# One run of transposes between an expert's gate and up products

## The chip, the cores and the metric

The kernel runs on one core of a Trainium2 chip. The metric is the time of one execution on the device, in microseconds. The core has five engines that run side by side, each with a queue of its own that it works off in order: TensorE (PE; its weight loads have a row of their own, PEld), VectorE (DVE), ScalarE (ACT), GpSimd (POOL) and SyncE (SP). DMA engines move data between the memory of the chip and the core's own buffers. TensorE writes to PSUM, from where ACT and DVE read.

## The reference

The input has 8192 tokens of 512 numbers. It is normalised, and two things are added to it: a random-feature attention, which is two dense products with an exponential in between, and a mixture of experts with 64 experts, of which each token takes 8, and one shared expert.

```python
xn = layernorm(x)
# attention: random features of the tokens times those of the weights
feats = rfs(xn, xis, exp(xis), proj_matrix)
y = einsum('bsr,or->bso', feats, rfs(input_weights, xis, exp(xis), proj_matrix))
# experts: the first CAP = 256 tokens that chose expert e, in order
dispatch = zeros((E, CAP, h)).at[flat_e, pos_c].add(tokens[tidx] * valid[:, None])
g = einsum('ech,ehi->eci', dispatch, gate_w)
u = einsum('ech,ehi->eci', dispatch, up_w)
expert_out = einsum('eci,eih->ech', silu(g) * u, down_w)
output = zeros((t, h)).at[tidx].add(expert_out[flat_e, pos_c] * topk_w * SCALE * valid)
output += (silu(tokens @ shared_gate_w) * (tokens @ shared_up_w)) @ shared_down_w
return x + y + output
```

All of it is in float32. The gate and up weights of an expert are 512 x 256 each, the down weights 256 x 512.

## The kernel before

**Precision.** Each factor of a product is split in two: a high part that ACT makes as a rounded copy (`upper`, line 98), and a low part that DVE makes as the difference (`rest`, line 101). `products` (line 103) then issues three rounds of matmuls into the same PSUM tile: high by high, high weight by low value, low weight by high value. The low part of the weights is thus needed last, by the last third of the matmuls.

**Stages.** A first stage goes through the even blocks of 512 tokens: normalisation, transposes, routing, shared expert and attention. Then the loop over the experts begins (line 931). After it the last block and the shared expert of the odd blocks are computed (`ends`, line 892).

**The loop over the experts.** In step `i` the following is written down, in this order:

- the loads of the gate and up weights of expert `i+2` and of the down weights of `i+1` (SP);
- `hidden(i)` (line 792): the gate products, 48 matmuls of 256 columns, then the up products, 48 more, in PSUM tiles `ps_gu`; then `gated` (line 497), which is a tanh on ACT (499) and two multiplications on DVE (500, 501) into `sg`; then the split of `sg` into `ehT`;
- one step of `slots`, which finds the tokens of later experts; `gather(i+4)`, two indirect DMAs that POOL issues and that fetch the rows of that expert's 256 tokens into `xg`;
- `turn_slots(i+1)` (line 762): the 256 gathered tokens of the next expert are turned, in eight transposes of 128 x 128 on TensorE, in two halves with a PSUM tile `ps_t` each; ACT and DVE split each half into `gT`. Then DVE computes the tokens' shares `we` (781, 785);
- `split_gates(i+1)`: the gate and up weights of the next expert into `gu_h` and `gu_l`;
- some steps of `late_attention` (line 577), the attention of the odd blocks, which is put between the experts (tiles `ps_fu`, `ps_y`, `fU`, `yb`);
- `down(i-1)` (line 810): the down products of the expert before, in tiles `ps_e`, and the addition of its rows to the output by indirect DMA;
- `split_down(i)`.

**What sets the order.** The order in which the lines are written isn't the order in a queue. A scheduler puts the instructions of each engine in a fixed order when the program is built: earlier lines go first, but what it believes not to be ready is passed over for something later that is. The order can be bound by hand with `behind(a, b)` (line 117), which says that `a` comes after `b`, and adds no wait where both are on the same engine. The dictionary `last` keeps such instructions: `last["pe"]` is the newest matmul of `products`. In the kernel before, only the transposes of expert 0 are bound in this way.

**Buffers.** The tiles of 4 KiB per partition (weights, their parts, `gT`, `ehT`, `fU` and more) share a pool `four` of 40; `xg` has 4 buffers, `ps_t` 2, and `ps_gu` and `ps_e` share 4.

Of the kernel before, what the change touches and what calls it, by code (L numbers as in the profile page):

```python
# [22 lines left out]
E = 64  # L23
# [30 lines left out]
def rfs_attention_moe_kernel(  # L54
# [29 lines left out]
    def kib4(shape, name, dt=FPR):  # L84
        return four.tile(shape, dt, tag="four", name=name)
# [11 lines left out]
    def upper(dst, src):  # L97
        return nc.scalar.copy(dst, src)  # L98

    def rest(dst, src, hi, on=nc.vector):  # L100
        return on.tensor_tensor(dst, src, hi.bitcast(FP), ALU.subtract)  # L101

    def products(ps, w, v, start, stop):

        n = len(w)
        for part, (a, b) in enumerate(((0, 0), (0, 1), (1, 0))):
            for c in range(n):
                last["pe"] = nc.tensor.matmul(  # L108
                    ps,
                    w[c][a],  # L110
                    v[c][b],
                    start=(start and part == 0 and c == 0),
                    stop=(stop and part == 2 and c == n - 1),
                )
        return last["pe"]

    def behind(a, b):

        tc.add_manual_dep(a.ins, b.ins.name, ORDER, reason="what a needs comes late")
# [45 lines left out]
    last = {}  # L165
# [323 lines left out]
    def projected(v, rc, ps):  # L489
        products(ps, parts(pT, KC, ts(rc, P)), v, True, True)  # L490
# [6 lines left out]
    def gated(dst, g, u):  # L497

        nc.scalar.activation(dst, g, AF.Tanh, scale=0.5)
        nc.vector.scalar_tensor_tensor(dst, dst, 1.0, g, ALU.add, ALU.mult)  # L500
        nc.vector.scalar_tensor_tensor(dst, dst, 0.5, u, ALU.mult, ALU.mult)  # L501
# [9 lines left out]
    def attended(po, fT, s, start):  # L511

        return products(po, parts(fT, RC, ts(s, P)), parts(fW, RC), start, True)

    def dense(b, xT, whole, w, rows_of):
# [6 lines left out]
        for ic in range(IC):  # L522
            gu = []
            for n in range(2):
                ps = ps_mm.tile([P, TB], FP, tag="mm", name="ps_gu")
                wn = [(sgu_h[n][:, c, ts(ic, P)], sgu_l[n][:, c, ts(ic, P)]) for c in range(KC)]
                products(ps, wn, v, True, True)
                gu.append(ps)
            g, u = gu
            r = act.tile([P, TB], FP, tag="t", name="r")  # L530
            gated(r, g, u)
            upper(hT[0][:, ic, :], r)
            last["dve"] = rest(hT[1][:, ic, :], r, hT[0][:, ic, :])
            yield
# [111 lines left out]
    def split_gates(gu):  # L646
        return list(zip(*(split(t, "gu") for t in gu)))

    def split_down(d):
        return split(d, "d")  # L650
# [88 lines left out]
    def load_gates(e):  # L739
        gu = [kib4([P, KC, I], "gu", FP) for _ in range(2)]  # L740
        for t, w in zip(gu, (gw, uw)):
            nc.sync.dma_start(t, w[e].rearrange("(c p) i -> p c i", p=P))
        return gu

    def load_down(e):
        d = kib4([P, IC, H], "d", FP)
        nc.sync.dma_start(d, dw[e].rearrange("(c p) h -> p c h", p=P))
        return d

    def gather(e):  # L750
        xgs[e] = rows.tile([P, NH, XW], FP, tag="xw", name="xg")
        for h in range(NH):
            in_turn(
                nc.gpsimd.indirect_dma_start(  # L754
                    out=xgs[e][:, h, :],
                    out_offset=None,
                    in_=xnw,
                    in_offset=bass.IndirectOffsetOnAxis(ap=who[:, e, h : h + 1], axis=0),
                )
            )  # L760

    def turn_slots(e):
        xg = xgs.pop(e)
        xr = xg.bitcast(FPR)
        gp = [kib4([P, KC, CAP], "gT") for _ in range(2)]
        for c2 in range(KC // 2):
            pr = ps_tr.tile([P, 2, CAP], FPR, tag="tr", name="ps_t")
            ps = pr.bitcast(FP)
            for c in range(2):
                for h in range(NH):  # L770
                    turned_s = nc.tensor.transpose(  # L771
                        pr[:, c, ts(h, P)], xr[:, h, ts(c2 * 2 + c, P)], ident_r
                    )
                    if e == 0:
                        behind(turned_s, last["pe"])
            cs = slice(2 * c2, 2 * c2 + 2)
            upper(gp[0][:, cs, :], ps)
            turned_r = rest(gp[1][:, cs, :], ps, gp[0][:, cs, :])

        we = rt.tile([P, NH], FP, tag="we", name="we", bufs=4)  # L780
        shares = nc.vector.scalar_tensor_tensor(
            we, xg[:, :, H + e], 1.0, xg[:, :, H + E], ALU.add, ALU.mult
        )
        behind(shares, turned_r)
        nc.vector.reciprocal(we, we)
        wes[e] = we
        if e == 0:

            last["dve"] = shares
        return gp  # L790

    def hidden(e, gp, w):
        hi, lo = w
        v = [(gp[0][:, c, :], gp[1][:, c, :]) for c in range(KC)]
        gu = []
        for n in range(2):
            ps = ps_mm.tile([P, IC, CAP], FP, tag="mm", name="ps_gu")
            for ic in range(IC):
                wn = [(hi[n][:, c, ts(ic, P)], lo[n][:, c, ts(ic, P)]) for c in range(KC)]
                products(ps[:, ic, :], wn, v, True, True)  # L800
            gu.append(ps)
        g, u = gu
        sg = act.tile([P, IC, CAP], FP, tag="t", name="sg")
        gated(sg, g, u)
        hp = kib4([P, 2, IC, CAP], "ehT")
        upper(hp[:, 0], sg)
        last["dve"] = rest(hp[:, 1], sg, hp[:, 0])
        return hp

    def down(e, hp, w):  # L810
        dh, dl = w
        group = []
        ye = yes[e % len(yes)]
        for h in range(NH):
            po = ps_mm.tile([P, H], FP, tag="mm", name="ps_e")
            products(
                po,
                [(hp[:, 0, c, ts(h, P)], hp[:, 1, c, ts(h, P)]) for c in range(IC)],
                [(dh[:, c, :], dl[:, c, :]) for c in range(IC)],
                True,  # L820
                True,
            )
            nc.scalar.activation(ye[:, h, :], po, AF.Copy, scale=wes[e][:, h : h + 1])  # L823
            now = nc.gpsimd.indirect_dma_start(  # L824
                out=out,
                out_offset=bass.IndirectOffsetOnAxis(ap=who[:, e, h : h + 1], axis=0),
                in_=ye[:, h, :],
                in_offset=None,
                compute_op=ALU.add,
            )  # L830
            group.append(now)

        chain(group)
        in_turn(*group)

    xgs, wes, gps, gates, downs, gws, dws, hps = ({} for _ in range(8))
# [45 lines left out]
    for n in range(NS):  # L882
        next(rest_of)
        if n == 0:
            next(slots)
            gws[0] = split_gates(gates.pop(0))
    rest_steps -= RC + NS
    gps[0] = turn_slots(0)
    next(slots)
    yes = [kib4([P, NH, H], "ye", FP) for _ in range(3)]  # L890
# [40 lines left out]
    for i in range(E + 1):  # L931


        if i + 2 < E:
            gates[i + 2] = load_gates(i + 2)
        if i + 1 < E:
            downs[i + 1] = load_down(i + 1)
        if i < E:
            hps[i] = hidden(i, gps.pop(i), gws.pop(i))
        next(slots, None)  # L940
        if i + 4 < E:
            gather(i + 4)
        if i + 1 < E:
            gps[i + 1] = turn_slots(i + 1)
            gws[i + 1] = split_gates(gates.pop(i + 1))
        for _ in range(rest_steps * i // E, rest_steps * (i + 1) // E):
            next(rest_of, None)
        if i >= E - 2:
            next(last_of)
        if i == E:  # L950

            next(last_of)
        if i > 0:
            down(i - 1, hps.pop(i - 1), dws.pop(i - 1))
        if i < E:
            dws[i] = split_down(downs.pop(i))
            if i == E - 2:

                last["down"] = last["split"]
# [40 lines left out]
```

## Time and profile before

| what | value |
|---|---|
| time, median of 3 runs | 1310.99 us (1310.63 to 1311.27) |
| the profiled execution | 1310.94 us, of which 1309.2 are the span from the first to the last instruction |
| transposes `ps_t` (line 771) | 512, median 246 ns each, from 425.7 to 1130.7 us |
| copies `gT` on ACT (line 98) | 128, median 588 ns |
| subtractions `gT` on DVE (line 101) | 128, median 682 ns |
| gathers `xg` | 128, 3.5 to 10.1 us to landing, median 7.1 |
| data moved by DMA | 338.61 MB, mean 259 GB/s |

The profile is of one execution. A row of a timeline gives the start and the length in microseconds, the engine, the line of the code, the operation, the tile written and those read, the shapes and the count of instructions that follow each other. The matmuls overlap, so the lengths are longer than the pitch at which they start; where TensorE is the question, the starts are to be compared. A row for weight loads (PEld) belongs to the matmuls beside it. A line of waits names who waited, for whom, how long in total, how often and the longest. Line 108 is the matmul of `products` and lines 98 and 101 are `upper` and `rest`, for whatever tile they are called, so the tiles tell the rows apart.

### The profile page before, as it was taken

What the parts mean: (1) busy time and instruction counts of PE and PEld (TensorE: products, weight loads), DVE (VectorE), ACT (ScalarE), POOL (GpSimd) and SP (SyncE); (2) the same over time, 40 slices, a digit from 0 to 9 for tenths busy, and PEclk for the clock granted to TensorE, in tenths of its full rate; (3) what the DMA queues carried; (4) which work ended last, traced back from release to release, by engine and by line L of the source; (5) the groups of instructions that cost most, each with busy time, mean ns of one, the idle gap of its engine ahead of it and who ended that gap; (6) DMA issues with size and microseconds to landing.
All of it is one profiled execution on the core that took longest, in us unless ns stands there. A gap on an engine that the chain in (4) does not pass through costs nothing.

```text
span 1309.2 us, 21368 instructions
## 1 busy us (share of the span) xinstructions
PE 1296.7 (99%) x7648; PEld 1138.6 (87%) x7648; DVE 925.0 (71%) x1922; ACT 645.2 (49%) x1017; POOL 581.7 (44%) x692
## 2 busy tenths in 40 slices
PE   8999999999999999999999999999999999999998
PEld 6888888888888999999999999999999999988886
DVE  7978768867865776777767677776776676643555
ACT  5643544354432555656566556555665566540111
POOL 3122022123106767877666667767676654210000
PEclk9999999999999999999999999999999999999999
DMA  7665675675586989999999999999999999784995
GB/s 255 242 213 205 244 279 199 238 286 212 201 307 193 317 226 330 259 290 272 304 282 266 292 272 274 246 321 262 282 256 303 280 261 233 206 239 168 318 319 193
DMA packets 189498, 338.61 MB, mean 259 GB/s; under 512 B 15952, under 2 KB 87632, under 8 KB 189392
## 3 DMA queue, kind: packets, MB, share of 16 engines
q1 hardware_dynamic: 153456, 245.93, 54.6%
q0 software_dynamic: 35936, 91.32, 29.7%
q8 instruction: 60, 0.98, 0.3%
q14 instruction: 46, 0.38, 0.1%
HBM read 220.66 MB, written 104.99 MB: 249 GB/s over the span
## 4 chain that ended last, share of the span: by engine, by line
PE 91%; DVE 4%; DMA 2%; SPq 1%; ACT 1%; issue 1%; POOL 0%; DVEq 0%; ACTq 0%
PE ps_gu L108 41%; PE ps_e L108 13%; PE ps_o L108 13%; PE ps_y L108 6%; PE ps_fu L108 6%; PE ps_f L108 4%; PE ps_t L771 3%; PE ps_x L331 2%; PE ps_l L364 2%; DMA xb<-in_L_attn_x_dram 1%; DVE st L275 1%; DMA xT_l<-turned 1%; SPq L262 1%; DVE xT_l L101 1%; DMA gu<-in_L_ffn_up_w_dram 0%
## 5 line engine op out<-in xcount | busy, mean ns | idle before, releaser
L824 POOL DMA_INDIRECT out_dram<-ye,who x128 | 225.3, 1760 | 189.3 <-ACT ye L823 140.9
L108 PE MATMUL ps_gu<-gT,gu_h 128*128 128x256 f32 x2048 | 290.0, 283 | 0.0
L108 PEld LDWEIGHTS ps_gu<-gT,gu_h 128*128 128x128 f32 x2048 | 267.2, 191 | 5.6 <-ACT gu_h L98 1.0
L701 POOL DMA_INDIRECT at<-upto,line x128 | 138.0, 1078 | 76.0 <-DVE first_of L695 37.3
L108 PE MATMUL ps_gu<-gT,gu_l 128*128 128x256 f32 x1024 | 167.0, 285 | 0.0
L101 DVE TENSOR_TENSOR gu_l<-gu,gu_h 128x1024 fp32r<-128x1024 f32 x128 | 155.7, 1218 | 6.9 <-ACT gu_h L98 6.9
L754 POOL DMA_INDIRECT xg<-xnw,who x128 | 137.3, 1073 | 39.0 <-issue 32.0
L108 PE MATMUL ps_e<-d_h,ehT 128*128 128x512 f32 x512 | 148.5, 391 | 0.0
L108 PEld LDWEIGHTS ps_gu<-gT,gu_l 128*128 128x128 f32 x1024 | 140.7, 191 | 0.3
L98 ACT CAST gu_h<-gu 128x1024 fp32r<-128x1024 f32 x128 | 132.4, 1058 | 0.0
L98 ACT CAST ehT<-sg 128x512 fp32r<-128x512 f32 x64 | 39.7, 621 | 156.3 <-DVE sg L501 156.3
L823 ACT ACTIVATE ye<-ps_e,we 128x512 f32<-128x512 f32 x128 | 88.6, 694 | 57.0 <-PE ps_e L108 56.1
L108 PEld LDWEIGHTS ps_e<-d_h,ehT 128*128 128x128 f32 x512 | 94.7, 188 | 18.8
L246 POOL TENSOR_TENSOR a<-rstd,ve 128x4 f32<-128x4 f32 x45 | 10.5, 233 | 200.1 <-DVE rstd L242 197.6
L501 DVE SCALAR_TENSOR_TENSOR sg<-sg,ps_gu 128x512 f32<-128x512 f32 x64 | 43.9, 686 | 68.4 <-PE ps_gu L108 68.0
L507 ACT ACTIVATE f<-f,ab 128x512 f32<-128x512 f32 x64 | 46.3, 723 | 82.0 <-DVE f L493 81.3
L101 DVE TENSOR_TENSOR d_l<-d,d_h 128x1024 fp32r<-128x1024 f32 x64 | 78.2, 1222 | 7.8 <-ACT d_h L98 7.4
L101 DVE TENSOR_TENSOR gT<-ps_t,gT 128x512 fp32r<-128x512 f32 x128 | 83.2, 682 | 0.2 <-ACT gT L98 0.2
L101 DVE TENSOR_TENSOR ehT<-sg,ehT 128x512 fp32r<-128x512 f32 x64 | 44.3, 692 | 51.5 <-ACT ehT L98 51.5
L108 PE MATMUL ps_o<-fW_h,fT 128*128 128x512 f32 x288 | 80.0, 392 | 0.2 <-ACT fT L98 0.2
L108 PE MATMUL ps_e<-d_l,ehT 128*128 128x512 f32 x256 | 79.3, 391 | 0.0
L108 PE MATMUL ps_o<-d_h,hT 128*128 128x512 f32 x256 | 79.1, 396 | 0.0
(181 smaller groups left out, 2526.8 us busy)
## 6 DMA issues: line engine op xcount, KB each, us to landing
gu<-in_L_ffn_gate_w_dram SPq DMA_DIRECT2D x64, 512.0 KB
gu<-in_L_ffn_up_w_dram SPq DMA_DIRECT2D x64, 512.0 KB
d<-in_L_ffn_down_w_dram SPq DMA_DIRECT2D x64, 512.0 KB
xnw<-xw SPq DMA_DIRECT2D x32, 577.0 KB
xb<-in_L_attn_x_dram SPq DMA_DIRECT2D x32, 512.0 KB
out_dram<-xb SPq DMA_DIRECT2D x32, 512.0 KB
xT_h<-turned SPq DMA_DIRECT2D x30, 512.0 KB
xT_l<-turned SPq DMA_DIRECT2D x30, 512.0 KB
```

The lines of the kernel that those rows point to most:

```text
L98: return nc.scalar.copy(dst, src)
L101: return on.tensor_tensor(dst, src, hi.bitcast(FP), ALU.subtract)
L108: last["pe"] = nc.tensor.matmul(ps, w[c][a], v[c][b], start=(start and part == 0 and c == 0), stop=(stop and part == 2 and c == n - 1),)
L331: last["turn"] = nc.tensor.transpose(pr[:, ts(s, P)], src(s)[:, ts(kc, P)], ident if dt is FP else ident_r)
L364: logits = nc.tensor.matmul(pl, rwp[:, kc].rearrange("p t e -> p (t e)"), v[kc], start=(n == 0 and kc == 0), stop=(n == 1 and kc == KC - 1),)
L501: nc.vector.scalar_tensor_tensor(dst, dst, 0.5, u, ALU.mult, ALU.mult)
L507: nc.scalar.activation(f, f, AF.Exp, scale=ab[:, rc : rc + 1])
L701: nc.gpsimd.indirect_dma_start(out=at[:, e % TE, h, :], out_offset=None, in_=upto, in_offset=bass.IndirectOffsetOnAxis(ap=line[:, e, h : h ...
L754: nc.gpsimd.indirect_dma_start(out=xgs[e][:, h, :], out_offset=None, in_=xnw, in_offset=bass.IndirectOffsetOnAxis(ap=who[:, e, h : h + 1], ...
L771: turned_s = nc.tensor.transpose(pr[:, c, ts(h, P)], xr[:, h, ts(c2 * 2 + c, P)], ident_r)
L823: nc.scalar.activation(ye[:, h, :], po, AF.Copy, scale=wes[e][:, h : h + 1])
L824: now = nc.gpsimd.indirect_dma_start(out=out, out_offset=bass.IndirectOffsetOnAxis(ap=who[:, e, h : h + 1], axis=0), in_=ye[:, h, :], in_o ...
```

## The change

`turn_slots(e + 1)` is called from within `hidden(e)`, between the gate and the up products, and no longer from the loop. The first of its eight transposes is bound behind the last gate product; its last one is kept in `last["run"]`, and the next matmul that `products` issues, which is the first up product, is bound behind it. With the transposes the copies and subtractions of `gT` and the shares `we` are written down at the earlier place, ahead of `gated`. For expert 0, only the first transpose is now bound behind the product before it, and not all eight.

```diff
@@ products
                     stop=(stop and part == 2 and c == n - 1),
                 )
+                if "run" in last:
+                    behind(last["pe"], last.pop("run"))
         return last["pe"]
@@ turn_slots
                     turned_s = nc.tensor.transpose(
                         pr[:, c, ts(h, P)], xr[:, h, ts(c2 * 2 + c, P)], ident_r
                     )
-                    if e == 0:
+                    if c2 == c == h == 0:
+
                         behind(turned_s, last["pe"])
             cs = slice(2 * c2, 2 * c2 + 2)
             upper(gp[0][:, cs, :], ps)
             turned_r = rest(gp[1][:, cs, :], ps, gp[0][:, cs, :])
+        last["run"] = turned_s
@@ hidden
             gu.append(ps)
+            if n == 0 and e + 1 < E:
+                gps[e + 1] = turn_slots(e + 1)
@@ the loop over the experts
         if i + 1 < E:
-            gps[i + 1] = turn_slots(i + 1)
             gws[i + 1] = split_gates(gates.pop(i + 1))
```

## The prediction

> **What bounds the kernel.** First the page: the busy shares, the clock row and the chain of waits.
>
> ```profile
> span 1309.2 us, 21368 instructions
> PE 1296.7 (99%) x7648; PEld 1138.6 (87%) x7648; DVE 925.0 (71%) x1922; ACT 645.2 (49%) x1017; POOL 581.7 (44%) x692
> ...
> PEclk9999999999999999999999999999999999999999
> ...
> PE 91%; DVE 4%; DMA 2%; SPq 1%; ACT 1%; issue 1%; POOL 0%; DVEq 0%; ACTq 0%
> ```
>
> TensorE sets the end, at its full clock, so a microsecond counts only if it leaves TensorE's queue. Next the windows, cut where the experts begin and end (columns: length, busy time and count of each engine, granted clock, DMA share, GB/s):
>
> ```profile
> 0.00:427.00 427.00, 419.94 (x2058) 348.22 (x2058) 322.70 (x1018) 189.34 (x354) 104.69 (x331) 1.00 0.67 237
> 427.00:1142.00 715.00, 715.00 (x4883) 658.05 (x4883) 517.18 (x780) 424.05 (x615) 470.81 (x358) 1.00 0.98 275
> 1142.00:1309.20 167.20, 161.73 (x710) 132.29 (x708) 85.14 (x124) 31.77 (x49) 6.20 (x4) 0.99 0.74 243
> ```
>
> The change acts in the middle stretch alone (64 experts, about 11.9 us each), where TensorE shows no idle time at all. The time left to gain hides in the pitch of its instructions, from start to start. From the timeline I take the usual pitch: 227 ns for a matmul of 512 columns, 120 ns for one of 256. At these prices, and 84 ns per transpose (below), everything TensorE starts in this stretch comes to 707.3 us of its 714.9: only about 7.6 us are lost, and the change can't win more.
>
> **The price of a run.** TensorE's timeline around experts 18 and 19 (start, length, what, count):
>
> ```profile
> 631.62 0.64 PE L108 MATMUL ps_gu<-gT,gu_l 128*128 128x256 f32 x4
> 632.10 0.80 PE L771 MATMUL ps_t<-ident_r,xg 128*128 128x128 f32 x8
> 632.74 1.16 PE L108 MATMUL ps_y<-fW_h,fU 128*128 128x512 f32 x4
> 633.74 1.08 PE L108 MATMUL ps_y<-fW_l,fU 128*128 128x512 f32 x4
> ...
> 638.28 1.12 PE L108 MATMUL ps_gu<-gT,gu_h 128*128 128x256 f32 x8
> 639.24 0.46 PE L771 MATMUL ps_t<-ident_r,xg 128*128 128x128 f32 x4
> 639.53 0.72 PE L108 MATMUL ps_gu<-gT,gu_l 128*128 128x256 f32 x4
> ```
>
> Eight transposes start at 632.10 and the next row at 632.74: 80 ns each. But the four matmuls behind them take 1.00 us to the next row, where four at 227 ns take 0.91. Leaving a run costs something: the first matmul behind it holds the queue for about 300 ns instead of 227 (or 190 instead of 120), while the first two transposes of a run are cheap (60 ns each).
>
> I counted the rows of ps_t from 425.9 to 1131 us: 111 for 64 experts (32 of eight, 41 of four, 16 of two, 10 of one, 8 of three, 2 of six, 2 of seven). For each I took the time from its first transpose to the fifth matmul after its end, less 120 or 227 ns per matmul. A straight line through these gives 84 ns per transpose plus 51 ns per run. Over 84 ns each, the 111 runs lose 5.84 us in all: an eight followed by 512 columns 56 ns (32 of them, 1.80 us), a four followed by 256 columns 22 ns in the median (358 ns in all), the rest being waits that fall into the same places. What is lost away from the runs is 1.75 us.
>
> **The change, part by part.** Nothing is computed that wasn't before: 512 transposes, 128 copies and 128 subtractions stay. No DMA is moved and nothing passes SP's or POOL's queue.
>
> *The runs.* With the transposes of expert e+1 fixed behind the gate products of e and ahead of its up products, 111 runs become 64. An eight followed by 256 columns isn't in the trace. By the four that is followed by 256 columns it is 358 + 4 x 84 = 694 ns, 22 over; by the eight followed by 512 columns it is 56 over. So the 64 lose 1.4 to 3.6 us, and the gain is 5.84 - 1.4 = 4.4 to 5.84 - 3.6 = 2.2 us. I take 22 ns, as what follows a run sets the price of leaving it and in the new place 256 columns follow; rounded, **4.3 us**.
>
> *The cover that goes.* In 23 experts a run of one half stands just ahead of the gate's first use of gu_l (639.24 above), and that is no accident. VectorE's timeline there:
>
> ```profile
> 636.97 1.28 DVE L101 TENSOR_TENSOR gT<-ps_t,gT 128x512 fp32r<-128x512 f32 x2
> 638.17 0.15 DVE L781 SCALAR_TENSOR_TENSOR we<-xg 128x2 f32<-128x2 f32 x1
> 638.24 1.22 DVE L101 TENSOR_TENSOR gu_l<-gu,gu_h 128x1024 fp32r<-128x1024 f32 x1
> ```
>
> The weights' low half is ready at 639.46, after the run began at 639.24: the transposes fill a wait of 0.22 us. Over the 23 these waits sum to 2.6 us, and some 0.06 us of hand-over each makes 4.0. The new order bars transposes there. Two ends: it costs 4.0 us if the split stays as late, and it wins up to 0.9 us, the uncovered waits that nine other experts show at this place (six of 41 to 82 ns) or at the gate's first products (three of about 180 ns), if the splits come earlier. I take 0: the three VectorE rows ahead of the split (1.28 + 0.15, all of the transposed tokens) move some 3 us forward with the transposes (the second half of a run starts 3.0 us or more behind the gate's last product in most experts), far more than the longest wait.
>
> *The moved copies.* Two ACT copies (588 ns each) and on VectorE two subtractions (682), the shares (152) and the reciprocal (157) come before the gate and up results are used: 1.67 us of VectorE per expert. The view of waits says what room there is:
>
> ```profile
> ACT ehT L98 <- DVE sg L501: 151.2, 57, 3.1
> ...
> DVE sg L501 <- PE ps_gu L108: 64.9, 51, 1.6
> ACT sg L499 <- PE ps_gu L108: 62.9, 49, 3.5
> ...
> DVE ehT L101 <- ACT ehT L98: 50.7, 58, 3.7
> ...
> DVE sg L500 <- ACT sg L499: 32.8, 25, 2.7
> ```
>
> VectorE idles 64.9 + 32.8 + 50.7 = 148 us here, 2.3 per expert, most of it while up is computed, which is when the moved work now comes. Where it doesn't fit, L500 and L501 are late by up to 0.7 us, and after them ehT; the down products that read it stand an iteration (11.9 us) later, so nothing on TensorE waits. Cost 0; without that cover it would be 0.7 us an expert.
>
> *The new waits.* Up products now stand behind the transposes in TensorE's queue, and behind up the late attention and the down products. The transposes wait for the gather of e+1, whose second half is issued at least 14.6 us (mostly 21 to 31) before the gate ends, against 3.5 to 10.1 us to landing. Expert 1 alone has 8.3 us: 0 by the median landing of 7.1, 1.8 us once by the longest. I take 0. The two gT buffers are held up to 3 us longer, out of 40 that the weight loads draw on as well; those loads are issued 17.6 us or more, mostly 20 to 30, ahead of their first use, so a delay of 3 us leaves 14: 0.
>
> [...] The trace holds 32 runs of eight already, and the clock in three of them, looked at alone, is 1.00, their pitch 80 to 88 ns. [...]
>
> The sum: the span goes from 1309.2 to 1304.9; the profiled execution took 1310.94 with what lies around the span, the median is 1310.99, so 1310.99 - 4.3 = **1306.7 us**.
>
> **Rivals.** *The split comes early and its waits go too:* 4.3 + 0.9 = 5.2, so 1305.8; for it, VectorE's new slack; against it, that the fixed order of its queue may use the slack otherwise. *A wait takes the gain's place:* the 23 covered waits come into the open for 4.0 us, or other work still falls between the transposes (only the first of them and the first up product are tied), so that there are as many runs as before: 1310.7 to 1311. For it, half of the splits end within 0.2 us of their use. *Slower:* VectorE executes in order; the subtractions of gT now wait for transposes, and what is queued behind them (yb, d_l, gu_l) waits as well. If the gate's low half then waits in every expert as long as in the 22 where it was late (2.6/22 + 0.06 = 0.18 us), that is 11.5 us against 4.3: 1318.2. It decides from (4.3 + 2.6)/64 = 0.11 us per expert on. Against it: 72% load on VectorE in this stretch, and work that moves forward rather than back.
>
> **How the numbers follow.** Forecast 0.40 (its own range 1306.0 to 1308.8), early split 0.17, gain eaten 0.25, slower 0.18. A measurement of this kernel can tell 0.2%, 2.6 us. The first two are faster but for a corner of the forecast's range: 0.55; the third is no change, with that corner 0.27; slower 0.18. The range takes in the first three: from 1304.5 (the 7.6 us of all losses, less the 1.4 that 64 runs keep, is 1304.8) to 1313.0 (the third with expert 1's wait of 1.8).
>
> **What would show it.** Right: about 64 rows of ps_t with eight each, each after a gate's last row; TensorE still without idle time; gu_l ending well ahead of its use; the stretch of the experts about 4 us shorter. Wrong: rows of ps_t in pieces; matmul pitches over 200 ns where gu_l begins; waits of TensorE for VectorE or for gathers, in the waits or the chain.

## The result and the profile after

The changed kernel takes 1309.28 us (median of 22 runs, 1307.85 to 1310.75) where the kernel before took 1311.12 in runs beside it: the ratio is 0.9985 (0.9979 to 0.9992), a gain of some 2 us. A second comparison gave 0.9989 (0.9982 to 0.9995). The gain is smaller than the 0.2% that the prediction called the least a measurement can tell, but both intervals exclude no gain at all. The forecast was 4.3 us, 1306.7. So the sign was right, and more than half of the expected gain is missing. The time lies outside the forecast's own range (1306.0 to 1308.8) and inside the whole range (1304.5 to 1313.0) only because that one also took in a gain that is eaten up.

One number of the kernel's description has to be corrected first: the gate products of an expert are 24 matmuls and the up products 24, not 48 each. From here on the line numbers are those of the kernel that is shown; they shift by a few lines from one to the next.

The page of the changed kernel:

```profile
span 1308.0 us, 21401 instructions
PE 1295.1 (99%) x7648; PEld 1136.1 (87%) x7648; DVE 925.9 (71%) x1922; ACT 644.1 (49%) x1017; POOL 587.0 (45%) x692
```

The profiled execution took 1309.75 us, 1.2 less than the one of before; the pair of profiles thus shows less than the medians do. The experts' stretch, cut at its own ends (window, length, busy and count of each engine, clock, DMA), before and then changed:

```profile
427.10:1141.90 714.80, 714.80 (x4882) 657.88 (x4882) 517.09 (x780) 423.95 (x615) 470.77 (x357) 1.00 0.98 275
427.50:1140.80 713.30, 713.24 (x4883) 655.49 (x4883) 518.00 (x780) 422.88 (x615) 475.94 (x358) 1.00 0.98 276
```

The kernel before took 714.8 us for one instruction of TensorE less. The order that the change asked for is there. TensorE's timeline around one turn of the changed kernel:

```profile
541.84 0.64 PE L108 MATMUL ps_gu<-gT,gu_l 128*128 128x256 f32 x4
542.32 0.80 PE L773 MATMUL ps_t<-ident_r,xg 128*128 128x128 f32 x8
```

There are 64 rows of ps_t, each of eight, and each but expert 0's stands right behind a gate's last product. By the measure of the prediction (84 ns a transpose, 120 or 227 a matmul; what the stretch takes beyond that is lost) the losses divide so:

| lost in the experts' stretch, us | before | changed |
|---|---|---|
| at the runs of transposes | 5.84 (111 runs) | 2.09 (64 runs) |
| away from them | 1.75 | 4.25 |
| sum | 7.59 | 6.34 |

The places of the runs gave 3.75 us. Not all of that is the price of a run: before, the medians (50 ns where 512 columns follow, 75 runs; 25 ns where 256 do, 36 runs) come to 4.65 us, and the other 1.2 us were waits that fell into the same places. And 2.5 us came back somewhere else. The timeline of TensorE shows where, at the start of expert 10's gate in the changed kernel:

```profile
538.54 0.39 PE L108 MATMUL ps_y<-fW_h,fU 128*128 128x512 f32 x1
538.89 1.22 PE L108 MATMUL ps_gu<-gT,gu_h 128*128 128x256 f32 x8
539.95 0.63 PE L108 MATMUL ps_y<-fW_h,fU 128*128 128x512 f32 x2
```

A matmul of 512 columns holds the queue for 0.227 us, but the gate starts 0.35 us after it, and its eight products take 1.06 us to the next row, not 0.96. That is 0.23 us lost, though no row of TensorE is marked as idle: the wait sits in the weight loads. What they wait for is on ACT:

```profile
532.23 1.07 ACT L98 CAST gT<-ps_t 128x512 fp32r<-128x512 f32 x2
536.70 0.69 ACT L830 ACTIVATE ye<-ps_e,we 128x512 f32<-128x512 f32 x1 [3.40 <-PE ps_e L108]
537.28 0.61 ACT L98 CAST ehT<-sg 128x512 fp32r<-128x512 f32 x1
537.79 1.05 ACT L98 CAST gu_h<-gu 128x1024 fp32r<-128x1024 f32 x1
```

The high half gu_h of the gate's weights is done at 538.84, and the gate starts 0.05 us later. ACT could have made it long before: it stood idle for 3.40 us at ye, the scaled copy of the down products, waiting for ps_e, with ehT and gu_h queued behind. The loads aren't what it waits for; they are issued 18 us or more ahead of their use, as before. Counted at every gate's first products, such waits come to 2.3 us in 13 experts; before they were 0.65 us in four, and some more inside the places of the runs. In nine experts of the changed kernel a ye stands between the copies gT and the gate's gu_h, as here; seven of them have a wait of 0.23 us.

The view of waits says the same in sums (who, for whom, total, times, longest). Before:

```profile
ACT ye L823 <- PE ps_e L108: 53.2, 41, 4.8
...
DVE gu_l L101 <- ACT gu_h L98: 6.9, 25, 0.9
...
PEld ps_gu L108 <- ACT gu_h L98: 1.0, 3, 0.3
```

Changed:

```profile
ACT ye L830 <- PE ps_e L108: 81.3, 54, 5.9
...
DVE gu_l L101 <- ACT gu_h L98: 13.4, 44, 0.9
...
PEld ps_gu L108 <- ACT gu_h L98: 4.7, 15, 0.4
```

ACT waits half as long again for ps_e, and what needs gu_h waits more for it. Of the waits that the prediction wanted to use as room, the two around ehT are smaller, while VectorE waits no less for ps_gu; so a part of the room was used, but in an order that puts ye ahead. In the changed kernel:

```profile
ACT ehT L98 <- DVE sg L503: 112.0, 44, 2.8
...
DVE sg L503 <- PE ps_gu L108: 72.0, 59, 2.3
...
DVE ehT L101 <- ACT ehT L98: 26.1, 27, 1.9
```

### The profile page after: what moved, and what is told of

Its sections match the earlier page's. It is cut to its first block, busy times and chain, and to the rows that moved or that the text cites. A ratio compares the mean times of both kernels' runs of the same rounds, so it can differ in the third digit from the quotient of the medians.

```text
span 1308.0 us, 21401 instructions
## 1 busy us (share of the span) xinstructions
PE 1295.1 (99%) x7648; PEld 1136.1 (87%) x7648; DVE 925.9 (71%) x1922; ACT 644.1 (49%) x1017; POOL 587.0 (45%) x692
## 4 chain that ended last, share of the span: by engine, by line
PE 87%; DVE 7%; DMA 3%; SPq 1%; issue 1%; ACT 1%; POOL 0%; ACTq 0%; DVEq 0%
PE ps_gu L108 41%; PE ps_e L108 13%; PE ps_o L108 12%; PE ps_fu L108 6%; PE ps_y L108 5%; PE ps_t L773 3%; PE ps_f L108 3%; PE ps_x L333 2%; PE ps_l L366 1%; DMA xb<-in_L_attn_x_dram 1%; DVE st L277 1%; DVE f L495 1%; SPq L264 1%; DVE xT_l L101 1%; DVE fT L101 1%
## 5 line engine op out<-in xcount | busy, mean ns | idle before, releaser
L831 POOL DMA_INDIRECT out_dram<-ye,who x128 | 232.7, 1818 | 181.5 <-ACT ye L830 120.8
L703 POOL DMA_INDIRECT at<-upto,line x128 | 131.9, 1030 | 76.0 <-DVE first_of L697 37.3
L756 POOL DMA_INDIRECT xg<-xnw,who x128 | 141.7, 1107 | 40.0 <-issue 30.0
L501 ACT ACTIVATE sg<-ps_gu 128x512 f32<-128x512 f32 x64 | 38.2, 597 | 77.7 <-PE ps_gu L108 77.7
```

The source lines that it names most:

```text
L703: nc.gpsimd.indirect_dma_start(out=at[:, e % TE, h, :], out_offset=None, in_=upto, in_offset=bass.IndirectOffsetOnAxis(ap=line[:, e, h : h ...
L756: nc.gpsimd.indirect_dma_start(out=xgs[e][:, h, :], out_offset=None, in_=xnw, in_offset=bass.IndirectOffsetOnAxis(ap=who[:, e, h : h + 1], ...
L831: now = nc.gpsimd.indirect_dma_start(out=out, out_offset=bass.IndirectOffsetOnAxis(ap=who[:, e, h : h + 1], axis=0), in_=ye[:, h, :], in_o ...
```

## The experiments

The theories, by the letters used below. A: each run of transposes has a price, which depends on what follows it. C (against it): the gain comes from the copies and subtractions that moved forward. D: what is missing is the gate's wait for gu_h behind ye on ACT. B and I: what is laid in front of gu_l, transposes (B) or late attention (I), covers a wait. E, F, G, H and J are the rivals that the expectations name. Each comparison is with the kernel before, run beside it on the same chip.

### The weights' wait

**e4_gate_before_ye**: the changed kernel, ye bound behind the high half of the next gate's weights, on ACT.

```diff
+        last["high"] = both[0]
...
-        return list(zip(*(split(t, "gu") for t in gu)))
+        gate = split(gu[0], "gu")
+        last["gate_high"] = last["high"]
+        return list(zip(gate, split(gu[1], "gu")))
...
-            nc.scalar.activation(ye[:, h, :], po, AF.Copy, scale=wes[e][:, h : h + 1])
+            behind(
+                nc.scalar.activation(ye[:, h, :], po, AF.Copy, scale=wes[e][:, h : h + 1]),
+                last["gate_high"],
+            )
```

> The changed kernel with one tie more on ACT: the copies ye of the down products come behind the high half of the next gate's weights. Theory D: ACT no longer stands idle for ps_e with gu_h queued behind; the waits of the gate's first products go, 2.3 us less than the changed kernel, about 1307. Rival E: the wait is only moved, since ye comes later and with it the PSUM of the down products: 1309 or more.

Measured: 1306.04 us, ratio 0.9965 (0.9952 to 0.9979). ACT at the same expert:

```profile
534.30 0.62 ACT L98 CAST ehT<-sg 128x512 fp32r<-128x512 f32 x1 [2.78 <-DVE we L792]
534.83 1.04 ACT L98 CAST gu_h<-gu 128x1024 fp32r<-128x1024 f32 x1
535.77 0.69 ACT L834 ACTIVATE ye<-ps_e,we 128x512 f32<-128x512 f32 x1
```

gu_h is now done at 535.87, 0.9 us ahead of the gate (536.75). ye starts 1.0 us ahead of the gate and no longer 2.2, and no new loss shows that would come from it. The sums of the waits follow:

```profile
ACT ye L834 <- PE ps_e L108: 40.2, 42, 2.3
...
PEld ps_gu L108 <- ACT gu_h L98: 0.3, 1, 0.3
```

The losses away from the runs fall from 4.25 to 1.33 us, those at the runs stay (1.81), and the stretch loses 3.1 us in all. Theory D holds for the changed kernel.

**e11_tie_again** and **e12_change_again**: the same kernel and the changed kernel side by side on one chip.

> The changed kernel with the ACT tie once more, beside the changed kernel on the same chip: by theory D 2.5 to 3.5 us below it.

> The changed kernel once more, as the base of the other three: 1.5 to 2.3 us below the kernel before, as it was measured.

Measured: 1306.11 us, 0.9968 (0.9956 to 0.9979), and 1308.87, 0.9989 (0.9982 to 0.9995). The intervals don't meet: the tie is worth 2.8 us, as expected.

**e5_before_tie**: the tie on the kernel before.

> The kernel before with the ACT tie alone (ye behind the next gate's high half), the transposes left where they were. Theory D (the tie mends a wait that the change brought in): before has only some 0.6 us of waits at the gate's first products, and its 111 runs stay, so 0 to 1 us less, 1310 to 1311. Rival F (the tie is worth as much without the change): 3.5 us less, as it was on the changed kernel, about 1307.

Measured: 1310.68 us, 0.9999 (0.9991 to 1.0007), with 113 runs of transposes and 7.7 us lost in the stretch. The tie alone is worth nothing there, and rival F falls. The order on ACT says why: before, a ye stands between gT and gu_h in two experts alone, so there was next to nothing for this tie to move. (In eight experts of that kernel gu_h is ready less than 0.1 us ahead of the gate as well, always with gT, not ye, straight ahead of it; against 13 in the changed kernel.)

**e3_weights_too**: the split of the next gate and up weights at the new place as well.

```diff
                 gps[e + 1] = turn_slots(e + 1)
+                gws[e + 1] = split_gates(gates.pop(e + 1))
...
-        if i + 1 < E:
-            gws[i + 1] = split_gates(gates.pop(i + 1))
```

> The changed kernel with the split of the next expert's gate and up weights moved to the same place, behind the transposes. Theory D (what was not gained is the gate waiting for its weights' high half, which ACT makes late because it stands idle in order): the waits at the gate's first products, 10 experts with 0.23 us each, and at its first use of gu_l, go: 2 to 3 us less than the changed kernel, about 1307. Rival E (the waits only move: ACT and VectorE come late with sg and the shared buffers are held longer): no gain or some loss, 1309 to 1312.

Measured: 1306.91 us, 0.9975 (0.9967 to 0.9983). It mends the wait in another way: the losses away from the runs are 1.74 us, and in 63 of 64 experts nothing stands in front of the gate's first gu_l any more, since the split is early. **e8_weights_and_tie**, both together:

> The changed kernel with both repairs, the weights' split at the earlier place and the ACT tie. Theory D: both mend the same wait, so the two together give little more than the tie alone: 1305.5 to 1306.5. Rival: they mend different waits and add up, 1303.5 to 1304.5.

Measured: 1307.08 us, 0.9974 (0.9963 to 0.9985); losses of 1.73 us away from the runs, as in e3. They don't add up, as they would if they mended different waits. The time is slightly above the expected range. The tie alone has the lowest median, but the intervals of e3, e4, e8 and e11 overlap.

### The price of a run

**e10_eight_runs**: on e4, the transposes one by one, each behind three gate products. The last has the place that it has in one run and the others are earlier, so nothing can come late for it.

```diff
...
+                if turning is not None and (part * n + c) % 3 == 2:
+                    next(turning, None)
...
```

> The changed kernel with the ACT tie, and the eight transposes one by one, each behind three gate products, the last behind the gate's last: every transpose is earlier than in one run, so none of the work behind them can be late for it. Theory A (leaving a run has a price of about 20 ns over, by the medians of the twos, fours and eights followed by 256 columns): 512 x 20 ns = 10.2 us instead of 1.6, so 8 to 9 us over the kernel with the tie (1306.0), 1314 to 1315. Rival H (runs have no price, the gain was waits): 1306 to 1307.

Measured: 1316.48 us, 1.0049 (1.0036 to 1.0063), 10.4 above e11. TensorE's timeline:

```profile
605.62 0.52 PE L108 MATMUL ps_gu<-gT,gu_h 128*128 128x256 f32 x3
605.98 0.22 PE L778 MATMUL ps_t<-ident_r,xg 128*128 128x128 f32 x1
606.04 0.57 PE L108 MATMUL ps_gu<-gT,gu_h 128*128 128x256 f32 x3
606.45 0.22 PE L778 MATMUL ps_t<-ident_r,xg 128*128 128x128 f32 x1
```

From 605.98 to 606.45 there are 0.47 us for one transpose and three matmuls, which alone take 0.36: 0.11 us for a transpose, where 84 ns is the price within a run. The 504 runs of one lose 12.4 us, 24.6 ns each; a run of eight followed by 256 columns loses 25.6 in the changed kernel. So leaving a run has the same price for one as for eight. Away from the runs only 1.25 us are lost. Theory A holds, rival H falls; so does C as the only cause, since here the copies come no later and the time rises with the number of runs. The expected 8 to 9 us were a little low, as I had taken 20 ns.

**e7_four_runs**: on e4, four runs of two, behind each quarter of the gate and up products.

> The changed kernel with the ACT tie, and the eight transposes in four runs of two, one behind each quarter of the gate and up products. Theory A (each run has a price): 256 runs instead of 64; by the twos of before 21 to 27 ns over for those followed by 256 columns, 30 to 50 for those followed by 512, so about 3 x 24 + 40 = 112 ns per expert instead of 26: 5.5 us more than the kernel with the tie (1306.0), 1311.5. Rival H (a run has no price of its own, the gain was waits): no more than 1 us over 1306.

Measured: 1318.41 us, 1.0055 (1.0041 to 1.0068), some 12 above e4 and 7 above theory A's number; rival H's is missed by more. A run of two has a median of 189 ns, 21 over, as expected; but the runs' places lose 11.3 us in all and others 4.0. The last pair comes behind the up products and the copies of gT with it, which is a likely reason but not tried. One wait of 2.3 us for gu_h is among the losses, and the mean clock of the profiled execution is 0.998, not 0.999 as before. The run doesn't separate price and waits, and that is why e10 was made.

**e2_moved_untied**: the changed kernel without its two ties.

```diff
-                    if c2 == c == h == 0:
+                    if e == 0:
                         behind(turned_s, last["pe"])
...
-        last["run"] = turned_s
```

> The changed kernel without its two ties: the transposes, copies and subtractions are written down between gate and up, and the scheduler may put them anywhere. Theory A: the time follows the number of runs: if they stay 64 eights, as in the changed kernel, 1309.3; each run more costs about 22 to 50 ns, so with 110 runs about 2 us more, 1311. Theory C (moved copies): the gain stays, 1309.3, whatever the number of runs.

Measured: 1308.63 us, 0.9985 (0.9978 to 0.9992): the same as with the ties. There are 83 runs, 45 of them of eight, so the move alone brings most of them together. They lose 4.4 us, and 2.3 are lost elsewhere, 6.7 in all: the ties win at the runs what they lose at the gate's weights. By the time alone this is nearer to C, and A's price for 19 more runs doesn't show in it; the split of the losses agrees with A.

This run also bears on theory D. gT is written down as far forward as in the changed kernel, and ACT waits nearly as long at ye, but the weight loads wait 0.5 us for gu_h and not 4.7:

```profile
ACT ye L829 <- PE ps_e L108: 76.2, 73, 4.0
...
PEld ps_gu L108 <- ACT gu_h L98: 0.5, 2, 0.3
```

A ye stands between gT and gu_h in three experts and not in nine. So the move alone doesn't bring most of the wait; the two ties on TensorE, with the move, changed the order that the scheduler gave to ACT.

**e1_run_old_place**: the ties alone, with the run at the old place, behind up.

```diff
+                if "run" in last:
+                    behind(last["pe"], last.pop("run"))
...
-                    if e == 0:
+                    if c2 == c == h == 0:
                         behind(turned_s, last["pe"])
...
+        last["run"] = turned_s
```

> The kernel before with the two ties alone: the eight transposes in one run at the old place, behind the up products. Theory A (a run has a price, and its place sets it): 64 runs, followed by 512 columns, so they lose about 64 x 56 ns = 3.6 us instead of 5.84; the stretch of the experts gains 2.2 us if nothing else changes, about 1309 us. Theory B (the transposes cover the wait for gu_l, and without them it comes into the open): up to 4.0 us back, about 1313. Theory C (the gain of the change comes from the copies and subtractions that were moved forward, not from the runs): no gain, 1311.

Measured: 1344.56 us, 1.0256 (1.0242 to 1.0270), and no theory had foreseen it. There are 64 runs of eight, but TensorE runs dry:

```profile
483.13 0.62 PE L108 MATMUL ps_e<-d_h,ehT 128*128 128x512 f32 x2
486.95 2.20 PE L108 MATMUL ps_gu<-gT,gu_h 128*128 128x256 f32 x10 [3.20 <-ACT gu_h L98]
```

ACT, at that place:

```profile
482.87 0.69 ACT L826 ACTIVATE ye<-ps_e,we 128x512 f32<-128x512 f32 x1 [2.55 <-PE ps_e L108]
483.79 0.69 ACT L826 ACTIVATE ye<-ps_e,we 128x512 f32<-128x512 f32 x1 [0.23 <-PE ps_e L108]
484.38 0.61 ACT L98 CAST ehT<-sg 128x512 fp32r<-128x512 f32 x1
484.88 1.07 ACT L98 CAST gT<-ps_t 128x512 fp32r<-128x512 f32 x2
485.84 2.01 ACT L98 CAST gu_h<-gu 128x1024 fp32r<-128x1024 f32 x2
```

It is the same kind of queue as in the changed kernel, and worse: both copies ye, then ehT, gT and only then gu_h. The stretch has six such waits of 3.0 to 3.6 us from start to start, some 20 us. And the wait shown costs more than itself, since the granted clock is lower around it. The window from 484 to 491 us, with a clock of 0.76 (third from the end):

```profile
484.00:491.00 7.00, 4.05 (x21) 4.05 (x22) 5.47 (x8) 4.80 (x7) 4.44 (x5) 0.76 1.00 295
```

The ten gate products from 486.95 take 2.0 us to the next row, 200 ns each on average and not 120. The mean clock of this execution is 0.991, that of the kernel before 0.999. As an estimate, the 0.008 between them are some 11 us of the 1345.7 us of the span. Together with the waits that is 31 of the 36.5 us by which this profiled execution is longer than that of the kernel before.

**e6_run_old_tie**: e1 with the ACT tie of e4.

> One run of eight at the old place, behind the up products, and the ACT tie. Theory D: the 34 us that the run at the old place lost come from ACT standing at ye with gT and gu_h queued behind; with the tie TensorE doesn't run dry there, and what is left is theory A's price, 64 runs followed by 512 columns: 1308 to 1310. Rival G (at the old place gT itself comes too late for the next gate, whatever ACT's order): still 1320 or more.

Measured: 1322.65 us, 1.0086 (1.0073 to 1.0100). The tie wins 22 of the 34 us, and the mean clock of the profiled execution is 1.0 and not 0.991. The rest remains: TensorE's weight loads still wait 13 times for gu_h, 8.3 us in all, though for gT itself only once, 0.5 us. So D's cause explains most of the loss, but its number is missed by 12 us; the number is rival G's, and its reason isn't seen as such. On ACT gu_h stands behind the copies gT here, which a run behind the up products makes late; that this is the rest was not tried.

### The cover

**e9_written_order**: the changed kernel with TensorE's products in the order in which they are written.

```diff
+                elif "strict" in last and part == 0 and c == 0:
+                    behind(last["pe"], last["strict"])
+        if "strict" in last:
+            last["strict"] = last["pe"]
...
+    last["strict"] = last["pe"]
```

> The changed kernel with TensorE's products in the order in which they are written: each group of products of the experts' loop is bound behind the last matmul of the group before, so that no late attention falls into a gate. Theory I (the wait for gu_l that the transposes covered is now covered by matmuls of the late attention, since the split is no earlier): in the changed kernel the 35 groups of late attention ahead of the gate's first gu_l cover 6.5 us of waits; with 0.06 us of hand-over each they come into the open, and the time goes up by some 5 to 9 us, to 1314 to 1318. Rival J (the split comes early enough, and the late attention stands there by chance): 1309 to 1310.

Measured: 1339.81 us, 1.0220 (1.0206 to 1.0234), 31 us above e12; both expectations were wrong in size. The waits of TensorE itself, of which the changed kernel shows none:

```profile
PE ps_gu L108 <- ACT gu_h L98: 13.3, 8, 2.4
...
PE ps_gu L108 <- DVE gu_l L101: 3.3, 6, 1.3
PE ps_e L108 <- DVE d_l L101: 2.7, 2, 1.4
```

The wait for gu_l comes into the open as theory I said (3.3 us on TensorE, 7.6 us in its weight loads), so theory I holds in kind. The larger part is gu_h: the order bars late attention at every place, not only ahead of gu_l, and the mean clock is 0.993, where the changed kernel has 0.999. As an estimate, these 0.006 of the span of 1339.0 us are some 8 us. This run thus shows that free filler covers waits, but not what the filler ahead of gu_l is worth alone.

## Why the prediction was right, and where it wasn't

The direction and the reason for the gain were right; the size was not. The gain of 1.8 us lies between the forecast (4.3) and the rival in which a wait takes the gain's place (0 to 0.3 us, given a chance of 0.25), and nearer to the rival.

**The bound** was right: TensorE sets the end, and only its pitch counts. In every version the losses in the experts' stretch account for the profiled time to within 1.3 us.

**The price of a run** was right. Forecast: 64 runs at 22 ns, 1.4 us left of 5.84. Measured: 63 at 25.6 ns, 1.61 us, and 0.47 at expert 0's run, where 0.36 us lie between the first transpose and the second. The step gave 3.75 us for the 4.3 that I put down (5.84 less 1.4 is 4.4). That a row which wasn't in the trace, eight followed by 256 columns, could be built from the fours followed by 256 was borne out by 694 ns worked out and 696 measured (median); e10 shows that each run has this price.

**"The cover that goes"** was put at 0, and that the 0 came out is luck: the reason given was wrong. I wrote that the split of gu_l would come three microseconds earlier. It doesn't: in 25 experts of the changed kernel it still ends after the place where it would be needed, by 6.7 us in sum (before, in 28 experts, 22 of them under a run of transposes). But in 35 experts, 24 of these among them, matmuls of the late attention stand there in place of the transposes. Expert 9's gate in the changed kernel:

```profile
528.20 1.12 PE L108 MATMUL ps_gu<-gT,gu_h 128*128 128x256 f32 x8
529.16 0.40 PE L108 MATMUL ps_y<-fW_h,fU 128*128 128x512 f32 x1
529.39 0.39 PE L108 MATMUL ps_y<-fW_l,fU 128*128 128x512 f32 x1
529.62 0.63 PE L108 MATMUL ps_gu<-gT,gu_l 128*128 128x256 f32 x4
530.10 1.12 PE L108 MATMUL ps_gu<-gT,gu_h 128*128 128x256 f32 x8
```

VectorE's two splits of gu_l take from 528.19 to 530.72 there, so the gate's is done at about 529.4, behind 529.16. The two matmuls in between fill that, and switching to them and back leaves the pitch at 227 and 120 ns. Before, the transposes that stood there had a price of their own (a four followed by 256 columns 22 ns in the median). The 0.06 us of hand-over that the prediction put on each wait is what the trace of before shows: where the gate waits for gu_l or gu_h, it starts as little as 53 to 55 ns behind the end of the split.

**"The moved copies ... Cost 0"** is the step that failed. It asked whether ACT and VectorE had room, and they had. The prediction went through VectorE's order in front of gu_l, but not through ACT's in front of gu_h, which gu_l itself is made from. "Nothing on TensorE waits" was then wrong: with gT moved forward and the run tied, the scheduler put ye, which waits for the down products, ahead of ehT and gu_h in nine experts (two before); ACT stands idle there, and the gate's first products wait. These waits are most of the missing 2.5 us: e4 takes them away with one tie and lands at 1306.0, near the 1306.7 of the forecast. e5 shows that the tie mends nothing before the change. e2 shows that moving gT without the ties on TensorE doesn't bring most of these waits; why the scheduler's order turns with them, no run shows.

**The new waits**: behind expert 0 the transposes wait for no gather; they start 0.1 us behind the gate's last product in all 63 experts. The buffers and the loads delay nothing.

**The clock** loses nothing by the runs: with 64 runs of eight it is 1.00 in the experts' stretch of the changed kernel (427.50 to 1140.80 us), as it was before with 32.

**The rivals.** "A wait takes the gain's place" had the right form, with gu_l named instead of gu_h, and came two thirds true: 2.5 of 3.75 us. "Slower" was not far off: a kernel that makes the same run behind up instead of ahead of it (e1) loses 34 us, and mostly by the mechanism that rival named, a queue worked off in order with something blocked at its head, on ACT (ye, 2.55 us in the place shown) instead of VectorE.

## What to carry to other kernels

- Where one engine is the bound and shows no idle time, read its pitch: here a matmul that follows a run of transposes holds the queue some 70 ns longer (190 for 120, 300 for 227), and such prices were most of what was left to gain.
- When work is moved forward on a helper engine, ask not only whether there is room but what now stands at the head of its queue, and what the bound engine needs from behind it. Here one tie on the order, with no work changed, was worth more (2.8 us) than the change itself (1.8).
- A tie on one engine can turn the order on another (e2 against the changed kernel), so the queues of all engines are to be read again after it.
- Work that fills a wait may be replaced by other filler for nothing (here at 227 and 120 ns a matmul, the usual pitch), as long as the order is left free to take it; ties on the bound engine take that freedom away (e9).

## What the runs showed of the hardware

- Leaving a run of transposes cost about 25 ns over a run's own pitch of 84 ns where 256 columns followed, for a run of one (24.6, e10) as for a run of eight (25.6, changed kernel), and about 50 where 512 followed (median of 75 runs before). In the runs of eight of the changed kernel it is made up of about 70 ns more on the matmul behind the run (190 for 120), less 45 ns on the first two transposes (60 and 64 for 84). In the runs of one of e10 that are shown the transpose takes 60 and the matmul behind it 170.
- Behind two long waits of TensorE its products started at a longer pitch. In e1, behind 3.20 us, the gate's first ten took 200 ns each and not 120, with a clock of 0.76 in the window of 7 us; in e9, behind 1.84 us, the first eight took 219 ns each (957.93 to 959.68). Over the whole execution the mean clock was 0.991 in e1, where TensorE waited 20.2 us for gu_h (8 times, 3.2 at the longest), 0.993 in e9 (13.3 us for gu_h, 8 times, 2.4), 0.998 in e7 (2.3 us, once) and 1.0 in e6 (4.2 us, 3 times, 2.7), against 0.999 before. Why e6 with its wait of 2.7 us kept the clock, no run shows.
- Such a wait can cost more than its length: in e1 the gate that is shown starts 3.37 us later than 227 ns for each of the two matmuls ahead of it would have it (483.13 to 486.95), and its first 22 products take 4.23 us (to 491.18) and not the 2.64 of 120 ns each, 1.59 us more. That is 1.5 times the wait.
